# A four-layer graph network on one core: LSTM gates by tanh alone on rows of twice the size, norms of the last two groups on ScalarE, three planner times longer, last stores tile by tile

## The chip, the cores and the metric

The kernel runs on one core of a Trainium2 chip. The metric is the device time in microseconds (us) of one execution. A comparison can tell about 0.2% (5 us) from no change. A core has TensorE (PE: matmuls, with PEld for the loads of their weights), VectorE (DVE), ScalarE (ACT), GpSimd (POOL), and SyncE (SP), which here issues nearly all DMAs. Each engine works through its own instructions in order and waits at semaphores for the others.

## The reference

The input x is 128 batches of 64 nodes with 256 features, so 8192 rows; adj is one 64 x 64 matrix. Four layers follow, each of the form x = layernorm(x + layer(x)), all in float32. Layer 0 is three graph convolutions with weights adj * adj; layer 1 a spectral convolution with the eigenvectors of a normalized Laplacian of adj; layer 3 attention over neighbours. The change touches layer 2 above all: two graph convolutions with relu, and then LSTMs over windows of p = 1 to 4 nodes, one after the other on the same rows:

```python
def _lstm_last(Wih, Whh, bih, bhh, xs):          # xs [windows, p, H]
    def step(carry, x_t):
        h, c = carry
        g = x_t @ Wih.T + h @ Whh.T + bih + bhh
        i, f, gg, o = jnp.split(g, 4, axis=-1)
        c = jax.nn.sigmoid(f) * c + jax.nn.sigmoid(i) * jnp.tanh(gg)
        h = jax.nn.sigmoid(o) * jnp.tanh(c)
        return ((h, c), None)
...
for p in range(1, 5):
    nw = Tv // p
    wins = h[:, :nw * p, :].reshape(Bv * nw, p, Hd)
    last = _lstm_last(Wih[p - 1], Whh[p - 1], bih[p - 1], bhh[p - 1], wins)
    h = h.at[:, jnp.arange(nw) * p + (p - 1), :].set(last.reshape(Bv, nw, Hd))
```

## The kernel before

The 8192 rows are 64 tiles of 128 rows (two batches each), held in SBUF as X for the whole run. A group is four tiles; there are 16 groups. The first phase (to about 860 us) computes layer 0 for all groups while the eigenvectors are found on DVE in between. The second phase takes every group through layers 1, 2 and 3. The change lies in the second phase, apart from a scaling of the LSTM biases (cbi) at the seam.

In the second phase three groups are under way at any time (WAYS). Each is a generator: it issues some matmuls with what belongs to them on the other engines, and yields the time at which it may go on. This time is not measured; it is a statement: `now`, the planner's own count of TensorE time, plus a constant. The constants are at L920: MOVE for a copy out of PSUM, NORM for a norm, CELL for a step of the LSTM by its number of columns, SOFT for a softmax. The loop at the end of the kernel function (L1195) takes the first group whose time has come, and if none has, it moves `now` to the earliest one. TensorE's order is this order exactly. On the other engines a scheduler orders the instructions at build time, and the engine then keeps to that order.

The steps that the change touches:

- `lstm` (L989) computes gates transposed: 128 gate columns on the partitions, the windows of eight batches along the free dimension (256, 168 or 128 columns). Two halves h, and for each the gates i, f, g, o. Each gate is a few matmuls into PSUM and one ScalarE activation with the bias (L1027): sigmoid, or tanh for g. VectorE then forms the cell (L1031, L1032, L1034), ScalarE its tanh (L1035), VectorE the new hidden row (L1037, or L1046 back into hT at the last step).
- `layer2` (L1053) makes hT by a relu (L1073), runs the five LSTM calls, transposes back (L1089) and adds to X (L1090), two tiles at a time. A norm of the pair follows.
- `norm_parts` (L542) is the norm: statistics on VectorE (L551, L552), the inverse root as a power on GpSimd (L553, L554), and the application, on VectorE (L564). In the last two groups (ENDING, 14 and 15) every second tile is applied on ScalarE instead (L562), for which GpSimd forms a negated product (L557, L558).
- `layer3` (L1095) transposes X, copies it out of PSUM (L1114 or L1117, and L1118), multiplies by dw, transposes back, forms scores (L1140), softmax with an exp on ScalarE (L1153), attention times values, the sum into X (L1170), a norm, and the store by SyncE (L1174). In the last two groups layer 3 runs as two parts of two tiles.

ScalarE needs the table of a function loaded before it runs: an ACT_TABLE_LOAD in the trace. Nothing in the kernel asks for it; it is placed at build time.

Of the kernel before, what the change touches and what calls it, by code (L numbers as in the profile page):

```python
# [11 lines left out]
AF = mybir.ActivationFunctionType  # L12
ALU = mybir.AluOpType
# [525 lines left out]
LEAD = 10  # L539


def norm_parts(tc, pool, x, half, shared=False):  # L542


    nc = tc.nc
    n = x.shape[1]
    st = pool.tile([P, n, 6], F32, name="ln_st")
    mv = pool.tile([P, n, 2], F32, name="ln_mv")
    rs = pool.tile([P, n], F32, name="ln_rs")
    for t in range(n):  # L550
        nc.vector.bn_stats(st[:, t, :], x[:, t, :])  # L551
        nc.vector.bn_aggr(mv[:, t, :], st[:, t, :])  # L552
    nc.gpsimd.tensor_scalar(rs, mv[:, :, 1], EPS, None, op0=ALU.add)  # L553
    nc.gpsimd.tensor_tensor(rs, rs, half[:, :n], ALU.pow)  # L554
    if shared:
        nm = pool.tile([P, n], F32, name="ln_nm")
        nc.gpsimd.tensor_scalar(nm, mv[:, :, 0], -1.0, None, op0=ALU.mult)  # L557
        nc.gpsimd.tensor_tensor(nm, nm, rs, ALU.mult)  # L558
    yield
    for t in range(n):  # L560
        if shared and t % 2:
            nc.scalar.activation(x[:, t, :], x[:, t, :], AF.Identity, bias=nm[:, t:t + 1], scale=rs[:, t:t + 1])  # L562
            continue
        nc.vector.tensor_scalar(x[:, t, :], x[:, t, :], mv[:, t, 0:1], rs[:, t:t + 1],  # L564
                                op0=ALU.subtract, op1=ALU.mult)
# [22 lines left out]
            [lambda t=t: apply(t) for t in range(2)])  # L588


def rows_norm(tc, pool, x, half, shared=False):
    for _ in norm_parts(tc, pool, x, half, shared):
        pass


# [1 line left out]
def kernel(  # L597
# [296 lines left out]
    V.tensor_reduce(rs_col, adst, AX.X, ALU.add)  # L894
    V.tensor_scalar(wide["c_b0"], wide["c_b0"], rs_col, None, op0=ALU.mult)
    V.tensor_add(cbi, cbi, cbh)
    phase_a.close()
    us = keep.tile([P, 1], F32, name="us")
    ub2 = wide["b_b2"]
# [18 lines left out]

    now[0] = due[0] = 0.0
    MOVE, MIXED, LIN, CONV, NORM, SOFT = 1.2, 1.2, 1.5, 1.8, 5.2, 5.2  # L920
    CELL = {256: 3.3, 168: 2.2, 128: 1.9}

    def turn(out, in_):
        PE.transpose(out, in_, ident)  # L924
# [28 lines left out]
        yield now[0] + MIXED  # L953
        return dst

    def norm(xs, t, ready, more=0.0, shared=False):
        rows_norm(tc, small, xs[:, t:t + 2, :], half, shared)
        ready.append(now[0] + NORM + more)

    def layer1(xs, ready):  # L960
        a = yield from mixed(xs, u2, ready)
# [25 lines left out]
        return ready  # L987

    def lstm(hT, p, first, nw):  # L989


        n = 8 * nw
        wi, wh, bias = wih[p - 1], whh[p - 1], cbi[:, p - 1, :]
        c = hs = None
        for t in range(p):
            rows = slice(first + t, first + t + (nw - 1) * p + 1, p)
            xt = [hT[:, k, rows, :] for k in range(2)]
            last = t == p - 1
# [12 lines left out]
            if t:  # L1011
                yield ready
            if p > 1 and not t:
                c = tl(pg, [P, 512], "c")[:, :2 * n].rearrange("p (h n) -> p h n", h=2)
            new = None if last else tl(pg, [P, 512], "hs")[:, :2 * n].rearrange("p (h n) -> p h n", h=2)
            for h, q in units:
                j = 2 * "ifgo".index(q) + h
                m = slice(j * P, (j + 1) * P)
                pp = ahead.get((h, q))
                if pp is None:  # L1020
                    pp = ps4()[:, :n]
                    for k in range(2):
# [4 lines left out]
                S.activation(gate[q][:, h, :], pp, AF.Tanh if q == "g" else AF.Sigmoid, bias=bias[:, j:j + 1])  # L1027
                if q == "g":
                    to = gate["g"][:, h, :] if t or p == 1 else c[:, h, :]
                    if t:  # L1030
                        V.tensor_mul(c[:, h, :], c[:, h, :], gate["f"][:, h, :])  # L1031
                    V.tensor_mul(to, gate["i"][:, h, :], gate["g"][:, h, :])  # L1032
                    if t:
                        V.tensor_add(c[:, h, :], c[:, h, :], to)  # L1034
                    S.activation(gate["i"][:, h, :], c[:, h, :] if p > 1 else to, AF.Tanh)  # L1035
                if q == "o" and not last:
                    V.tensor_mul(new[:, h, :], gate["o"][:, h, :], gate["i"][:, h, :])  # L1037
                if q == "o":
                    if h == 0:
                        yield now[0]  # L1040
                elif h == 1 or len(units) == 8:
                    yield now[0]
            if last:

                for h in range(2):
                    V.tensor_mul(hT[:, h, slice(first + p - 1, first + nw * p, p), :],  # L1046
                                 gate["o"][:, h, :].rearrange("p (w b) -> p w b", b=8),
                                 gate["i"][:, h, :].rearrange("p (w b) -> p w b", b=8))
            ready = now[0] + CELL[n]
            hs = new  # L1050
        return ready

    def layer2(xs, g, ready):  # L1053
# [31 lines left out]
        for t in range(0, 4, 2):  # L1085
            p = ps4((P, 2, D))
            for j in range(2):
                for k in range(2):
                    turn(p[:, j, k * P:(k + 1) * P], hb[:, k, (t + j) * P:(t + j + 1) * P])  # L1089
            V.tensor_add(xs[:, t:t + 2, :], p, xs[:, t:t + 2, :])  # L1090
            norm(xs, t, ready, shared=g in ENDING)
            yield now[0]
        return ready

    def layer3(xs, g, ready, first, nt):  # L1095
# [20 lines left out]
            with tc.high_priority(offset=1500):  # L1116
                V.tensor_copy(xT[:, 0, :], ps[0][:, :nt * P])  # L1117
# [46 lines left out]
        for t in range(0, nt, 2):  # L1164
# [87 lines left out]
```

## Time and profile before

| | before |
|---|---|
| median of three runs | 2550.1 us (2548.05 to 2553.39) |
| the profiled execution | 2548.97 us, span 2547.2 us |
| granted TensorE clock | 0.996 |
| busy: PE, DVE, ACT, POOL | 98%, 56%, 44%, 5% |
| ACT_TABLE_LOAD | 31, 1.28 us each |
| output stores | 32 of 256 KB |

The span runs from the first to the last instruction. In the lines shown, a group or a timeline row gives the engine, the line of the kernel, the operation, the tile written and the tiles read; `[1.01 <-POOL ln_rs L554]` is idle time of the engine just before, and what ended it. A busy time of PE is the time in which some matmul is under way; records of matmuls overlap one another. In the list of waits the three numbers are the total in us, how often, and the longest.

### The profile page before, as it was taken

What the parts mean: (1) busy time and instruction counts of PE and PEld (TensorE: products, weight loads), DVE (VectorE), ACT (ScalarE), POOL (GpSimd) and SP (SyncE); (2) the same over time, 40 slices, a digit from 0 to 9 for tenths busy, and PEclk for the clock granted to TensorE, in tenths of its full rate; (3) what the DMA queues carried; (4) which work ended last, traced back from release to release, by engine and by line L of the source; (5) the groups of instructions that cost most, each with busy time, mean ns of one, the idle gap of its engine ahead of it and who ended that gap; (6) DMA issues with size and microseconds to landing.
All of it is one profiled execution on the core that took longest, in us unless ns stands there. A gap on an engine that the chain in (4) does not pass through costs nothing.

```text
span 2547.2 us, 38989 instructions
## 1 busy us (share of the span) xinstructions
PE 2495.1 (98%) x15020; PEld 2190.4 (86%) x15020; DVE 1414.6 (56%) x5002; ACT 1122.8 (44%) x2727; POOL 130.4 (5%) x316
## 2 busy tenths in 40 slices
PE   9999999999999999999999999999999999999996
PEld 7788887888878889988989889889898898988995
DVE  6888777778884433444453544534535445353335
ACT  2344333433333344545454454444444545445444
POOL 0000000000000100000000000000000000000001
PEclk9999999999999999999999999999999999999998
DMA  6000000000000300000000000000000000000000
GB/s 219 1 1 1 1 1 1 1 1 1 1 1 1 116 1 1 9 9 1 9 9 1 9 1 10 9 1 10 8 2 9 1 9 9 1 9 1 1 1 25
DMA packets 24570, 32.09 MB, mean 13 GB/s; under 512 B 2112, under 2 KB 21312, under 8 KB 24384
## 3 DMA queue, kind: packets, MB, share of 16 engines
q1 hardware_dynamic: 24032, 29.32, 3.4%
q8 instruction: 118, 1.93, 0.3%
q14 instruction: 68, 0.56, 0.1%
q10 hardware_dynamic: 352, 0.28, 0.0%
HBM read 21.20 MB, written 8.39 MB: 12 GB/s over the span
## 4 chain that ended last, share of the span: by engine, by line
PE 87%; DVE 6%; ACT 3%; POOL 2%; issue 1%; DMA 1%; SPq 0%; POOLq 0%; ACTq 0%; DVEq 0%
PE ps L716 84%; POOL ln_rs L554 1%; DVE X L564 1%; PE ps L924 1%; ACT gates L1027 1%; DVE D L51 1%; DVE ln_st L551 1%; PE ps L1140 1%; ACT L1027 1%; ACT L1153 1%; DVE X L1090 1%; PE pc L93 1%; DMA X<-in_x_dram 1%; ACT att L1153 0%; DVE gates L1032 0%
## 5 line engine op out<-in xcount | busy, mean ns | idle before, releaser
L716 PE MATMUL ps<-w,wih 128*128 128x128 f32 (+2 forms) x4992 | 894.1, 319 | 1.7 <-DVE w L1046 1.7
L716 PEld LDWEIGHTS ps<-w,wih 128*128 128x128 f32 x4992 | 763.8, 191 | 50.8 <-issue 8.4
L1027 ACT ACTIVATE gates<-ps,cbi 128x128 f32<-128x128 f32 (+2 forms) x1248 | 500.6, 408 | 581.1 <-PE ps L716 576.3
L716 PE MATMUL ps<-hs,whh 128*128 128x128 f32 (+2 forms) x3072 | 542.2, 303 | 4.4 <-DVE hs L1037 4.3
L716 PEld LDWEIGHTS ps<-hs,whh 128*128 128x128 f32 x3072 | 453.9, 191 | 33.7 <-issue 11.0
L1032 DVE TENSOR_TENSOR gates<-gates 128x128 f32<-128x128 f32 (+2 forms) x256 | 89.4, 349 | 253.9 <-ACT gates L1027 253.9
L716 PE MATMUL ps<-aw,h 128*128 128x256 f32 x1024 | 227.2, 380 | 0.0
L716 PEld LDWEIGHTS ps<-aw,h 128*128 128x128 f32 x1024 | 193.0, 190 | 25.8 <-ACT h L725 0.5
L725 ACT ACTIVATE h<-h 128x512 f32<-128x512 f32 x128 | 80.6, 629 | 169.4 <-DVE h L51 169.3
L1035 ACT ACTIVATE gates<-c 128x128 f32<-128x128 f32 (+2 forms) x288 | 98.1, 341 | 109.3 <-DVE c L1034 103.4
L1031 DVE TENSOR_TENSOR c<-c,gates 128x128 f32<-128x128 f32 (+2 forms) x192 | 62.4, 325 | 107.8 <-ACT gates L1027 105.5
L716 PE MATMUL ps<-ss,tw 128*128 128x256 f32 x512 | 117.9, 380 | 0.0
L716 PE MATMUL ps<-ss,aw 128*128 128x256 f32 x512 | 117.3, 379 | 0.0
L716 PE MATMUL ps<-m,aw 128*128 128x256 f32 x512 | 117.1, 380 | 0.0
L1046 DVE TENSOR_TENSOR w<-gates 128x256 f32<-128x256 f32 (+2 forms) x160 | 59.3, 377 | 101.8 <-PE ps L716 62.9
L716 PE MATMUL ps<-aw,m 128*128 128x512 f32 x256 | 114.5, 593 | 0.2 <-DMA aw<-in_a_w_dram 0.2
L1037 DVE TENSOR_TENSOR hs<-gates 128x128 f32<-128x128 f32 (+2 forms) x192 | 62.7, 327 | 92.0 <-ACT gates L1035 52.4
L564 DVE TENSOR_SCALAR X<-X,ln_mv,ln_rs 128x256 f32<-128x256 f32 x184 | 68.1, 410 | 81.6 <-POOL ln_rs L554 81.6
L716 PEld LDWEIGHTS ps<-ss,aw 128*128 128x128 f32 x512 | 96.6, 190 | 12.8
L716 PEld LDWEIGHTS ps<-ss,tw 128*128 128x128 f32 x512 | 96.4, 190 | 12.8 <-issue 0.2
L716 PEld LDWEIGHTS ps<-m,aw 128*128 128x128 f32 x512 | 95.7, 190 | 12.5 <-issue 0.5
L553 POOL TENSOR_SCALAR ln_rs<-ln_mv 128x2 f32<-128x2 f32 x96 | 22.8, 238 | 1569.4 <-DVE ln_mv L552 1567.6
(294 smaller groups left out, 3128.8 us busy)
## 6 DMA issues: line engine op xcount, KB each, us to landing
out_dram<-X SPq DMA_DIRECT2D x32, 256.0 KB, 2.1
X<-in_x_dram SPq DMA_DIRECT2D x30, 256.0 KB, 6.0
wih<-in_c_ih_dram SPq DMA_DIRECT2D x4, 1024.0 KB, 7.0
aw<-in_a_w_dram SPq DMA_DIRECT2D x3, 1024.0 KB, 10.8
whh<-in_c_hh_dram SPq DMA_DIRECT2D x3, 1024.0 KB, 9.1
aw<-in_a_w_dram SPq DMA_DIRECT2D x1, 512.0 KB, 6.3
cw<-in_c_w_dram SPq DMA_DIRECT2D x2, 256.0 KB, 5.1
X<-in_x_dram ACTq DMA_DIRECT2D x1, 256.0 KB, 3.6
```

The lines of the kernel that those rows point to most:

```text
L51: return getattr(self.engine, name)(out, *args, **kw)
L93: PE.matmul(out, lhsT, rhs, start=True, stop=True)
L551: nc.vector.bn_stats(st[:, t, :], x[:, t, :])
L564: nc.vector.tensor_scalar(x[:, t, :], x[:, t, :], mv[:, t, 0:1], rs[:, t:t + 1], op0=ALU.subtract, op1=ALU.mult)
L716: PE.matmul(out, lhsT, rhs, start=start, stop=stop)
L725: S.activation(dst, src, AF.Relu)
L1027: S.activation(gate[q][:, h, :], pp, AF.Tanh if q == "g" else AF.Sigmoid, bias=bias[:, j:j + 1])
L1031: V.tensor_mul(c[:, h, :], c[:, h, :], gate["f"][:, h, :])
L1032: V.tensor_mul(to, gate["i"][:, h, :], gate["g"][:, h, :])
L1035: S.activation(gate["i"][:, h, :], c[:, h, :] if p > 1 else to, AF.Tanh)
L1037: V.tensor_mul(new[:, h, :], gate["o"][:, h, :], gate["i"][:, h, :])
L1046: V.tensor_mul(hT[:, h, slice(first + p - 1, first + nw * p, p), :], gate["o"][:, h, :].rearrange("p (w b) -> p w b", b=8), gate["i"][:, h ...
```

## The change

Sigmoid is written as (1 + tanh(z/2))/2, so that all gates are tanh. To spare the extra operations, the rows in hT, the hidden rows and the cell are held at twice their value: the relu gets a scale of 2, the biases of i, f and o are halved once, the gates' scales are 0.25 (i, f, o) and 0.5 (g), the products on VectorE become one instruction of the form (a + 1) * b, and the last sum into X takes half. In the last two groups ScalarE applies every norm whose `scalar` is set (that of layer 2 and that of layer 3), both tiles of the pair; before, it took one of the two. Three stated times grow: CELL for 256 columns from 3.3 to 3.8, the second norm of a pair by 0.8 (and by another 1.8 in layer 2 of the last two groups), and the copy at the start of layer 3 by 0.6. The stores of the last two groups are one per tile.

```diff
@@ norm_parts
-    if shared:
+    if scalar:
         nm = pool.tile([P, n], F32, name="ln_nm")
...
-        if shared and t % 2:
+        if scalar:
             nc.scalar.activation(x[:, t, :], x[:, t, :], AF.Identity, bias=nm[:, t:t + 1], scale=rs[:, t:t + 1])
             continue
@@ seam
     V.tensor_add(cbi, cbi, cbh)
+    for q in (slice(0, 4), slice(6, 8)):
+        V.tensor_scalar(cbi[:, :, q], cbi[:, :, q], 0.5, None, op0=ALU.mult)
@@ stated times
-    CELL = {256: 3.3, 168: 2.2, 128: 1.9}
+    CELL = {256: 3.8, 168: 2.2, 128: 1.9}
...
-        ready.append(now[0] + NORM + more)
+        ready.append(now[0] + NORM + more + (0.8 if ready else 0.0))
@@ lstm
-                S.activation(gate[q][:, h, :], pp, AF.Tanh if q == "g" else AF.Sigmoid, bias=bias[:, j:j + 1])
+                S.activation(gate[q][:, h, :], pp, AF.Tanh, bias=bias[:, j:j + 1], scale=0.5 if q == "g" else 0.25)
...
-                        V.tensor_mul(c[:, h, :], c[:, h, :], gate["f"][:, h, :])
-                    V.tensor_mul(to, gate["i"][:, h, :], gate["g"][:, h, :])
+                        V.scalar_tensor_tensor(c[:, h, :], gate["f"][:, h, :], 1.0, c[:, h, :], op0=ALU.add,
+                                               op1=ALU.mult)
+                    V.scalar_tensor_tensor(to, gate["i"][:, h, :], 1.0, gate["g"][:, h, :], op0=ALU.add, op1=ALU.mult)
                     if t:
-                        V.tensor_add(c[:, h, :], c[:, h, :], to)
-                    S.activation(gate["i"][:, h, :], c[:, h, :] if p > 1 else to, AF.Tanh)
+                        V.scalar_tensor_tensor(c[:, h, :], c[:, h, :], 0.5, to, op0=ALU.mult, op1=ALU.add)
+                    S.activation(gate["i"][:, h, :], c[:, h, :] if p > 1 else to, AF.Tanh, scale=0.5)
                 if q == "o" and not last:
-                    V.tensor_mul(new[:, h, :], gate["o"][:, h, :], gate["i"][:, h, :])
+                    V.scalar_tensor_tensor(new[:, h, :], gate["o"][:, h, :], 1.0, gate["i"][:, h, :], op0=ALU.add,
+                                           op1=ALU.mult)
...
@@ layer2
-            relu(hT[:, c, :, :].rearrange("p n b -> p b n"), as3(h, 8))
+            S.activation(hT[:, c, :, :].rearrange("p n b -> p b n"), as3(h, 8), AF.Relu, scale=2.0)
...
-            V.tensor_add(xs[:, t:t + 2, :], p, xs[:, t:t + 2, :])
-            norm(xs, t, ready, shared=g in ENDING)
+            V.scalar_tensor_tensor(xs[:, t:t + 2, :], p, 0.5, xs[:, t:t + 2, :], op0=ALU.mult, op1=ALU.add)
+            norm(xs, t, ready, 1.8 if t and g in ENDING else 0.0, scalar=g in ENDING)
@@ layer3
-        yield now[0] + MOVE
+        yield now[0] + MOVE + 0.6
...
-            nc.sync.dma_start(out_t[:, at:at + 2, :], x2)
+            if ending:
+                for j in range(2):
+                    nc.sync.dma_start(out_t[:, at + j, :], x2[:, j, :])
+            else:
+                nc.sync.dma_start(out_t[:, at:at + 2, :], x2)
```

The last step's product into hT (L1046) changes in the same way as that of the hidden row.

More of the change, by code (lines that the diff above doesn't have):

```diff
@@ L539, with norm_parts @@
 LEAD = 10
-def norm_parts(tc, pool, x, half, shared=False):
+def norm_parts(tc, pool, x, half, scalar=False):
     nc = tc.nc
@@ L588, in scalar_norm, with rows_norm @@
             [lambda t=t: apply(t) for t in range(2)])
-def rows_norm(tc, pool, x, half, shared=False):
-    for _ in norm_parts(tc, pool, x, half, shared):
+def rows_norm(tc, pool, x, half, scalar=False):
+    for _ in norm_parts(tc, pool, x, half, scalar):
         pass
@@ L954, in mixed, with norm @@
         return dst
-    def norm(xs, t, ready, more=0.0, shared=False):
-        rows_norm(tc, small, xs[:, t:t + 2, :], half, shared)
-        ready.append(now[0] + NORM + more)
+    def norm(xs, t, ready, more=0.0, scalar=False):
+        rows_norm(tc, small, xs[:, t:t + 2, :], half, scalar)
+        ready.append(now[0] + NORM + more + (0.8 if ready else 0.0))
     def layer1(xs, ready):
@@ L1045, in lstm @@
                 for h in range(2):
-                    V.tensor_mul(hT[:, h, slice(first + p - 1, first + nw * p, p), :],
-                                 gate["o"][:, h, :].rearrange("p (w b) -> p w b", b=8),
-                                 gate["i"][:, h, :].rearrange("p (w b) -> p w b", b=8))
+                    V.scalar_tensor_tensor(hT[:, h, slice(first + p - 1, first + nw * p, p), :],
+                                           gate["o"][:, h, :].rearrange("p (w b) -> p w b", b=8), 1.0,
+                                           gate["i"][:, h, :].rearrange("p (w b) -> p w b", b=8), op0=ALU.add,
+                                           op1=ALU.mult)
             ready = now[0] + CELL[n]
```

## The prediction

> **What bounds the kernel now.** I read the busy table and the slices of the page first, then the table by stretches, then who TensorE waited for, then the timeline around those waits.
>
> ```profile
> PE 2495.1 (98%) x15020; PEld 2190.4 (86%) x15020; DVE 1414.6 (56%) x5002; ACT 1122.8 (44%) x2727; POOL 130.4 (5%) x316
> ...
> 1400.00:1600.00 200.00, 197.70 (x1336) 179.52 (x1335) 90.98 (x255) 94.66 (x230) 10.43 (x22) 1.00 0.02 6
> 2500.00:2547.00 47.00, 25.58 (x163) 19.62 (x161) 24.65 (x88) 15.32 (x36) 8.88 (x26) 0.79 0.10 34
> ```
>
> TensorE is the bound from end to end; DVE and ACT have half their time free in the middle. Only what makes TensorE wait counts, and the end, where it is idle nearly half of the time. The columns of the stretches are PE, PEld, DVE, ACT, POOL, granted clock, DMA share, GB/s.
>
> ```profile
> PE ps L924 <- DVE X L564: 11.2, 11, 5.3
> PE ps L924 <- ACT att L1153: 4.8, 4, 2.4
> PE ps L716 <- DVE hs L1037: 4.3, 11, 1.5
> PE ps L716 <- DVE w L1117: 3.9, 9, 0.4
> ```
>
> [...] A matmul's record overlaps the wait, so I took the price of a wait from the starts of the matmuls in the trace: the distance to the next start, less the median distance of that width (0.112 us for 128 columns, 0.216 for 256, 0.429 for 512). So counted, TensorE loses 58.9 us: 15 before 900 us (the change hardly touches that), 21.9 from 900 to 2400, and 22.3 after 2400. Another 10.6 us lie between the last matmul group (2536.6) and the end of the span. From 1300 to 2230 us the loss repeats every 103.3 us (one group of four tiles): 0.66 on X by L564 (layer 3 transposes its second pair of tiles), 0.60 on w by L1117 (the copy after them), 0.38 on hs by L1037 (recurrent matmuls of 256 columns). Nine of each: 5.9 + 5.4 + 3.4 = 14.7 us.
>
> **Part 1, one table for all (the gates).** At 1116 to 1121 us the timeline has:
>
> ```profile
> 1117.81 0.84 ACT L1153 ACTIVATE att<-v 64x256 f32<-64x256 f32 x2
> 1118.67 0.42 ACT L1035 ACTIVATE gates<-c 128x256 f32<-128x256 f32 x1
> ...
> 1119.11 1.28 ACT L1027 ACT_TABLE_LOAD   x1
> ...
> 1120.40 0.47 ACT L1027 ACTIVATE gates<-ps,cbi 128x256 f32<-128x256 f32 x1
> 1120.91 0.42 DVE L1046 TENSOR_TENSOR w<-gates 128x256 f32<-128x256 f32 x1 [1.33 <-ACT gates L1027]
> ...
> 1121.39 0.84 PE L716 MATMUL ps<-w,wih 128*128 128x168 f32 x4 [1.68 <-DVE w L1046]
> ```
>
> The tanh of L1035 runs straight after the exp of L1153, with no load; the load comes with the next sigmoid of L1027. So tanh and exp live in one table, and without sigmoid the 15 loads at L1027 and 15 at L1153 fall to one: 29 x 1.283 = 37.2 us of ACT. Of this only what TensorE waited for is worth time. Here the load sits on the path: TensorE lost 1.84 us. The same chain stands behind 0.95 us at 1029.4 (load at 1026.12, then a gate, a relu and the eT copy of L1160) and behind each repeating 0.38 (load at 1417.86, gate at 1419.15, hs at 1419.66, TensorE at 1420.14). All are smaller than 1.28 except the first: 1.3 + 0.95 + 3.4 = 5.6, taken as 5.5.
> The Trainium skill (ScalarE: Activation LUTs, What ACT_TABLE_LOAD costs) puts a switch at about 2.66 us, the load and a drain of 1.38. The trace differs: at 2484.27 a gate ends, the load runs from 2484.28 to 2485.56, the exp starts at 2485.58. So 1.3 a switch. By the page the loads hold ACT for 77 us and not 37, which would explain stalls twice as long as those seen; I keep the trace.
> Per element a tanh costs what a sigmoid does as far as the rows show: L1027 is one row of both, 470 ns at 256 columns. The scales are immediates of instructions that exist already. On DVE about 1,120 TENSOR_TENSOR (the lines L1031 to L1046 and L1090) become SCALAR_TENSOR_TENSOR with an immediate. Bounds: nothing (the 64x64 rows have 211 ns against 214), or +55 ns as with a per-partition scalar (L1071 746 against L1061 691), 61 us of DVE that is 45% busy there. The nearer row is the one with an immediate, so 0; the other end puts 0.2 us on a step of the recurrence, inside its allowance. The two scalings of cbi are under 0.3 us each, at the seam near 860 us, long before a gate reads them: 0.
>
> **Part 2, three stated times.** They move nothing in the hardware; they change which group's matmuls TensorE takes next. +0.8 for the second norm of a pair answers the 0.66, MOVE + 0.6 answers the 0.60, CELL 3.8 for 3.3 answers the 0.38. While the planner holds a group back, two others fill TensorE, so a longer time costs nothing where another is able. But every later choice moves too: the order of the evacuations on DVE and ACT, and the psum and work buffers they free. Of 5.9 + 5.4 I take 70%, 8 us: bounds 11.3 and, with new waits of the same size, 0 or below.
>
> **Part 3, the end.** Columns of the timeline: start, length, instruction, in brackets the idle time before it.
>
> ```profile
> 2540.06 0.41 DVE L564 TENSOR_SCALAR X<-X,ln_mv,ln_rs 128x256 f32<-128x256 f32 x1 [1.01 <-POOL ln_rs L554]
> 2540.11 0.19 POOL L558 TENSOR_TENSOR ln_nm<-ln_nm,ln_rs 128x2 f32<-128x2 f32 x1
> 2540.34 0.60 ACT L562 ACTIVATE X<-X,ln_nm,ln_rs 128x256 f32<-128x256 f32 x1 [5.08 <-POOL ln_nm L558]
> 2540.39 0.74 DVE L551 BATCH_NORM_STATS2 ln_st<-X 128x6 f32<-128x256 f32 x2
> ```
>
> DVE's apply waits 1.01 us for POOL at the head of DVE's queue, and the next pair's statistics, whose data were there at 2539.05, start behind it. Now 8 applies (4 norms of layer 2, 4 of layer 3) leave DVE for ACT. POOL already issues its four instructions for these norms: +0. Cost: ACT's second apply comes some 0.5 us after the first (0.60 less overlap), and it needs nm, 0.24 us later than rs. Queued behind it on ACT are the gates of the other group and the next copies; ACT waits there for nm already, for the odd tile, so only the 0.5 is new.
> A rule speaks against it: ScalarE: Activation LUTs, Rules for kernel authors, wants multiplies and adds on VectorE. The rows agree on the price of one, 600 against 410 ns: by the rule 8 x 0.19 = 1.5 us are lost. But what ends the wait is the queue, not the duration:
> Last norm: statistics 1.34 earlier, then POOL bounds (first pair's nm ends at 2540.30, 1.46 for the next: 2541.8 against 2543.26), 1.4 earlier; +0.5 for the second apply; the last store moves half the bytes (256 KB went from 2544.8 to 2545.7: -0.45). SP gets 4 more DMA issues of 0.37, beside the second apply, and about 0.1 more closing waits. Net -1.2.
> Second pair of group 15 before layer 3: TensorE lost 5.48 at 2522.9. Its statistics (2519.78) stood behind two such applies (2516.25, 2519.45). Without them POOL bounds: three norms from 2515.03 at 1.46 end at 2519.4, the applies at 2520.0 and 2520.5 against 2522.8 and 2523.25: 2.8 earlier. And the planner, told +0.8 +1.8, now lets the first pair's dw matmuls (8 of 16, which took 5.1 us behind the transposes) go into the wait: another 1.2. Together -4.
> Loads in the tail: 2508.15 (TensorE lost 2.56) and 2484.28 with 2486.77 (lost 1.29): of these -2. Tail: 1.2 + 4 + 2 = 7.2.
>
> **Sum.** 5.5 + 8 + 7.2 = 20.7 us. The profiled execution took 2548.97 (span 2547.2, 1.8 around it): 2528.3. It stood 1.1 under the median of the three runs, so 2529.
>
> **Rivals.**
> A, the new order gives back what it takes: the 8 us are 0, other waits appear. For it: the waits at 1131.2 (1.67, hs behind L564 on DVE) and 2259.4 (2.48, w by L951 behind L564) show that DVE's queue is not in the planner's times. 2529 + 8 = 2537.
> B, the tail keeps its length: TensorE's order makes the second pair's chain start later, or ACT, with applies at the head of its queue, delays gates and exps: only 1 of 7.2 is left: 2535. For it: ACT waited 20.8 us in all for nm there, 8 times. Against: it had 5 us idle before the last ones.
> C, slower: the longer times lock the three groups into a repeating order in which two of the six norms of a group meet DVE's queue badly, as at 1131.2. Price 2 x 1.67 a group, ten groups: 33 us; less the 20.7: 2529 + 33 = 2562. It decides from 2.1 us of new wait a group. Against: the old order had only one repeating wait on L564, of 0.66.
> D, the loads stay, because the table of the first tanh lacks exp: the trace excludes it but for the choice made for the first one. Then 2529 + 7 = 2536.
>
> **Numbers.** Main case 0.56, A 0.2, B 0.12, D 0.02, C 0.06, and 0.04 for a mixture that ends at no change. [...] Faster 0.90, same 0.04, slower 0.06. Low end: all of the middle's 21.9 and half of the tail's 22.3 gone, 33: 2517. High end 2545: A and B together (2543) and the upper DVE price.
>
> **What would show it.** One or two ACT_TABLE_LOAD after the root's, and ACT some 37 us less busy. Waits of TensorE on w by L1117 and on hs by L1037 gone, those on X by L564 small in the middle; the windows of 200 us at 199 or more. L562 with 16 instead of 8 applies, L564 with 176; in the tail no DVE wait in front of statistics. PE's and POOL's busy time unchanged. Wrong: a repeating wait per group above 2 us, or a last stretch from 2400 us on as long as now.

## The result, and the profile after

| | before | after |
|---|---|---|
| median of four runs each | 2549.26 us (2548.05 to 2553.39) | 2540.14 us (2536.74 to 2541.67) |
| ratio | | 0.996 [0.9942, 0.9977] |
| profiled execution, span | 2548.97, 2547.2 | 2536.74, 2534.9 |

The change makes the kernel 9.1 us faster, where 21 was forecast. The profiled execution is the fastest of the four. It falls 12.3 us short of the span before; the sum had wanted 20.7.

The busy table and two stretches of the kernel after (columns of the stretches as before: PE, PEld, DVE, ACT, POOL, granted clock, DMA share, GB/s):

```profile
PE 2491.7 (98%) x15020; PEld 2188.7 (86%) x15020; DVE 1411.0 (56%) x4996; ACT 1094.8 (43%) x2706; POOL 133.1 (5%) x316
...
1400.00:1600.00 200.00, 197.28 (x1330) 179.37 (x1331) 91.13 (x257) 89.78 (x226) 10.85 (x23) 1.00 0.02 6
2500.00:2534.00 34.00, 19.61 (x138) 15.02 (x136) 18.61 (x66) 14.68 (x35) 7.97 (x24) 0.79 0.10 32
```

ACT was busy 28 us less: the 29 loads of 1.283 that went are 37.2, but the applications are busy 3.9 longer (8.7 for 4.8) and the gates 1.1; some 4 us are left without an explanation. The end is shorter: from 2500 us on 34.9 us are left where there were 47.2. But the stretch in the middle is no better: PE 197.28 of 200, where it was 197.70.

Groups of the kernel after, with the tables and the applications on ScalarE:

```profile
L562 ACT ACTIVATE X<-X,ln_nm,ln_rs 128x256 f32<-128x256 f32 x16 | 8.7, 592 | 9.5 <-POOL ln_nm L558 7.2 <-DVE ln_st L551 2.3
L674 ACT ACT_TABLE_LOAD x1 | 1.3, 1283 | 2.2 <-issue 2.2
L1030 ACT ACT_TABLE_LOAD x1 | 1.3, 1283 | 0.0
L1036 DVE SCALAR_TENSOR_TENSOR gates<-gates 128x256 f32<-128x256 f32 (+2 forms) x256 | 89.6, 350 | 294.6 <-ACT gates L1030 294.6
```

Two loads are left in the whole run: the root's and one for the gates. The product of the gates costs 350 ns with its immediate, 349 before.

What TensorE waited for in the kernel after, from 850 us on (total, times, longest). Lines have moved: L926 is the transpose that was L924, L1159 the exp (L1153), L1041 the hidden row (L1037), L1123 the copy in layer 3 (L1117), L953 the copy that was L951.

```profile
PE ps L926 <- DVE X L564: 17.2, 22, 1.1
PE ps L716 <- ACT v L1166: 3.3, 3, 2.0
PE ps L926 <- ACT att L1159: 3.2, 2, 1.8
...
PE ps L716 <- DVE hs L1041: 0.8, 1, 0.8
```

The repeating waits on w by the copy and on hs are gone, as forecast. Those on X by L564 were to get small; they doubled in number, from 11 to 22, and hold 17.2 us.

From here on TensorE's loss is counted by stages that are bounded by the same work in every kernel: the middle from about 919 to 2300 us, the tail from 2450 us to the last matmul group, and the piece behind that. The count is that of the prediction, from start to start. It is a net one (starts that come sooner than the median are set against the waits), so the single waits of a kernel can add up to more than its middle.

| us lost | middle | tail | behind the last matmuls |
|---|---|---|---|
| before | 22.1 | 22.5 | 9.6 |
| after | 20.4 | 14.6 | 7.9 |

So 9.6 of the 12.3 us came from the end and 1.7 from the middle; the remaining 1.0 lies ahead of the middle.

### The profile page after: what moved, and what is told of

Its sections match the earlier page's. It is cut to its first block, busy times and chain, and to the rows that moved or that the text cites. A ratio compares the mean times of both kernels' runs of the same rounds, so it can differ in the third digit from the quotient of the medians.

```text
span 2534.9 us, 38990 instructions
## 1 busy us (share of the span) xinstructions
PE 2491.7 (98%) x15020; PEld 2188.7 (86%) x15020; DVE 1411.0 (56%) x4996; ACT 1094.8 (43%) x2706; POOL 133.1 (5%) x316
## 4 chain that ended last, share of the span: by engine, by line
PE 93%; DVE 5%; POOL 1%; issue 1%; ACT 0%; DMA 0%; SPq 0%; ACTq 0%; POOLq 0%; DVEq 0%
PE ps L716 90%; PE ps L926 2%; POOL ln_rs L554 1%; DVE D L51 1%; DVE X L564 1%; DVE X L1096 1%; PE ps L1146 1%; PE pc L93 1%; DVE ln_st L551 1%; DVE tw L51 0%; POOL ln_rs L553 0%; DVE ln_mv L552 0%; DVE h L51 0%; DVE u L51 0%; DMA X<-in_x_dram 0%
## 5 line engine op out<-in xcount | busy, mean ns | idle before, releaser
L716 PE MATMUL ps<-w,wih 128*128 128x256 f32 (+2 forms) x4992 | 895.3, 319 | 0.0
L716 PEld LDWEIGHTS ps<-hs,whh 128*128 128x128 f32 x3072 | 453.0, 191 | 17.2 <-issue 1.7
L1036 DVE SCALAR_TENSOR_TENSOR gates<-gates 128x256 f32<-128x256 f32 (+2 forms) x256 | 89.6, 350 | 294.6 <-ACT gates L1030 294.6
L1034 DVE SCALAR_TENSOR_TENSOR c<-gates,c 128x128 f32<-128x128 f32 (+2 forms) x192 | 62.6, 326 | 117.7 <-ACT gates L1030 117.4
L1041 DVE SCALAR_TENSOR_TENSOR hs<-gates 128x128 f32<-128x128 f32 (+2 forms) x192 | 62.8, 327 | 89.1 <-ACT gates L1039 51.5
L564 DVE TENSOR_SCALAR X<-X,ln_mv,ln_rs 128x256 f32<-128x256 f32 x176 | 64.8, 410 | 81.0 <-POOL ln_rs L554 81.0
L1051 DVE SCALAR_TENSOR_TENSOR w<-gates 128x256 f32<-128x256 f32 (+2 forms) x160 | 59.5, 378 | 90.1 <-PE ps L716 61.0
```

What stands on the lines that cost most here:

```text
L716: PE.matmul(out, lhsT, rhs, start=start, stop=stop)
L1034: V.scalar_tensor_tensor(c[:, h, :], gate["f"][:, h, :], 1.0, c[:, h, :], op0=ALU.add, op1=ALU.mult)
L1036: V.scalar_tensor_tensor(to, gate["i"][:, h, :], 1.0, gate["g"][:, h, :], op0=ALU.add, op1=ALU.mult)
L1041: V.scalar_tensor_tensor(new[:, h, :], gate["o"][:, h, :], 1.0, gate["i"][:, h, :], op0=ALU.add, op1=ALU.mult)
L1051: V.scalar_tensor_tensor(hT[:, h, slice(first + p - 1, first + nw * p, p), :], gate["o"][:, h, :].rearrange("p (w b) -> p w b", b=8), 1.0, ...
```

## The experiments

Every kernel was timed beside the kernel before, in 5 to 20 executions; the median of before was 2552.1 to 2553.1 us. A gain in us is the distance of the ratio from 1, times that median.

| kernel | ratio to before | median | middle, as traced | drops of the clock in it | middle without them | tail | behind |
|---|---|---|---|---|---|---|---|
| e1_gates | 0.9955 [0.9942, 0.9967] | 2540.76 | 16.1 | 1 | 14.4 | 19.3 | 9.7 |
| e2_times | 0.9976 [0.9966, 0.9985] | 2545.13 | 20.2 | 0 | 20.2 | 20.6 | 9.7 |
| e3_tail | 0.998 [0.9973, 0.9987] | 2547.58 | 25.5 | 2 | 22.1 | 19.5 | 8.1 |
| e4_no_times | 0.9935 [0.9922, 0.9947] | 2535.07 | 16.0 | 1 | 14.3 | 16.0 | 8.0 |
| after_again | 0.9956 [0.9943, 0.9968] | 2540.35 | 20.4 | 0 | 20.4 | 16.4 | 8.2 |
| a1_old_cell | 0.9933 [0.9921, 0.9946] | 2536.22 | 16.2 | 0 | 16.2 | 14.0 | 8.0 |
| e5_tail_times | 0.993 [0.9918, 0.9943] | 2534.89 | 16.0 | 1 | 14.3 | 15.6 | 8.2 |
| b1_moved | 0.9936 [0.9922, 0.995] | 2534.21 | 18.3 | 1 | 16.6 | 13.8 | 8.0 |
| e6_loads | 1.002 [1.0012, 1.0029] | 2556.93 | 20.2 | 0 | 20.2 | 31.0 | 9.7 |
| e7_no_scalar | 0.9952 [0.9939, 0.9964] | 2540.19 | 16.1 | 1 | 14.4 | 19.8 | 8.9 |
| b2_split | 0.9936 [0.9922, 0.9949] | 2535.92 | 15.4 | 1 | 13.7 | 16.9 | 8.0 |
| b3_spaced | 0.9921 [0.9907, 0.9934] | 2531.27 | 7.6 | 0 | 7.6 | 19.6 | 8.2 |

The drops belong to single executions and not to a kernel; they are told of at the end, and each costs 1.7 us. The profiled execution of before had none in its middle.

### The parts, each alone

e1_gates is the kernel before with the gates by tanh and nothing else.

```diff
-  S.activation(gate[q][:, h, :], pp, AF.Tanh if q == "g" else AF.Sigmoid, bias=...)
+  S.activation(gate[q][:, h, :], pp, AF.Tanh, bias=..., scale=0.5 if q == "g" else 0.25)
...
```

> The kernel before with the gates by tanh alone (rows twice as large, all scales), nothing else of the change. TensorE's order is that of before. Theory T (the loads on TensorE's path are worth their waits, the stated times are worth nothing in the middle): the waits of 1.84 at 1121, 0.95 at 1029 and the repeating 0.38 on hs go, the repeating 0.66 and 0.60 stay, and about 2 us go in the tail: 7 us less, ratio 0.997. Rival R (the loads are hidden behind other groups, and the change's gain comes from the times and the tail): under 2 us, ratio 1.000.

Measured: 11.5 us faster (0.9955), more than the 7 expected; 14.4 in the middle instead of 22.1. The repeating wait on hs and the lone ones at 1029 and 1121 are gone. What TensorE waited for from 900 to 2450 us:

```profile
PE ps L926 <- DVE X L564: 4.6, 9, 0.5
PE ps L716 <- DVE w L1123: 3.9, 9, 0.4
PE ps L716 <- DVE w L953: 2.4, 1, 2.4
PE ps L716 <- DVE hs L1041: 1.5, 1, 1.5
```

By the spans of the profiled executions the gain is 8.2. The rest comes from the execution of before that was profiled: at 2548.97 us it lies 3.4 under the median of before.

e2_times is before with the three stated times.

```diff
-    CELL = {256: 3.3, 168: 2.2, 128: 1.9}
+    CELL = {256: 3.8, 168: 2.2, 128: 1.9}
-        ready.append(now[0] + NORM + more)
+        ready.append(now[0] + NORM + more + (0.8 if ready else 0.0))
-            norm(xs, t, ready, shared=g in ENDING)
+            norm(xs, t, ready, 1.8 if t and g in ENDING else 0.0, shared=g in ENDING)
-        yield now[0] + MOVE
+        yield now[0] + MOVE + 0.6
```

> The kernel before with the three stated times alone (CELL 3.8, second norm +0.8 and +1.8, MOVE + 0.6). The prediction's step: 8 us less, the repeating waits on X and w gone. Theory T (with the longer times all three groups are held back at once, TensorE has nothing to take): X waits of 1.25 and 0.64 in every group as in the kernel after, so nothing gained in the middle (0 to 3 us more, hs waits by table loads included), and 2 to 3 us gained in the tail by the other order: within 3 us of before, ratio 0.999 to 1.001.

Measured: 6.1 us faster (0.9976), so the expected "within 3 us of before" was missed, and the 8 of the prediction too. In the profile the gain is 1.9 in the middle and 1.9 in the tail, and the expected waits on X are there, 22 of them, 17.2 us in all, as in the kernel after. The timed gain is larger mainly because of the executions that were profiled: that of before lies 3.4 us under its median, at a mean clock of 0.996 where the executions at 0.994 took 2552.8 us and more, and that of e2_times lies 1.0 above its own.

e3_tail is before with the applications of the last two groups on ScalarE and the stores tile by tile.

```diff
-        if shared and t % 2:
+        if shared:
-            nc.sync.dma_start(out_t[:, at:at + 2, :], x2)
+            if ending:
+                for j in range(2):
+                    nc.sync.dma_start(out_t[:, at + j, :], x2[:, j, :])
+            else:
+                nc.sync.dma_start(out_t[:, at:at + 2, :], x2)
```

> The kernel before with ScalarE applying both tiles in the norms of the last two groups and the last stores tile by tile; times and gates as before. The prediction's step: last norm -1.2, second pair of group 15 -2.8, so 4 us less, ratio 0.9984; the wait of 5.5 us before layer 3's last transposes falls to under 3. Rival: ACT's queue delays gates and exps of the other group by as much; no change (1.000).

Measured: 5.1 us faster (0.998): 3.0 in the tail and 1.5 behind the last matmuls. The longest wait ahead of layer 3's last transposes is 2.4, as expected.

e4_no_times is after with the three old times, so e1 and e3 together.

```diff
-    CELL = {256: 3.8, 168: 2.2, 128: 1.9}
+    CELL = {256: 3.3, 168: 2.2, 128: 1.9}
-        ready.append(now[0] + NORM + more + (0.8 if ready else 0.0))
+        ready.append(now[0] + NORM + more)
-            norm(xs, t, ready, 1.8 if t and g in ENDING else 0.0, scalar=g in ENDING)
+            norm(xs, t, ready, scalar=g in ENDING)
-        yield now[0] + MOVE + 0.6
+        yield now[0] + MOVE
```

> The kernel after with the three stated times put back to those of before (gates, ScalarE norms and stores stay). Theory T: the middle has the old repeating waits of 0.66 and 0.60 (1.26 a group) in place of 1.25 and 0.64 (1.89), so 6 us less in the middle than the kernel after, and 2 to 3 us lost in the tail by the old order: 2536 to 2539, ratio to before 0.9955. Rival R (the times carry the gain): within 3 us of before, ratio 0.999.

Measured: 2535.07 us, 0.9935: 16.6 faster than before, which is 11.5 and 5.1. Gates and tail add up. The kernel without the longer times beats the one with them.

### The change again, and one time less

after_again is the changed kernel, unaltered.

> The kernel after, unchanged, beside the others of this call on one chip: ratio 0.996 as before. Theory T reads it against e4_no_times: the two orders differ by 0.0025, and this run should stand above the three others of this call.

Measured: 0.9956 against the 0.9935 of e4: the three times cost 5.4 us once the gates are tanh. In the profiles the middle has 20.4 against 14.3. With the old gates it was 20.2 (e2_times) against 22.1: with the longer times the middle loses the same, whichever the gates.

a1_old_cell takes only CELL back.

```diff
-    CELL = {256: 3.8, 168: 2.2, 128: 1.9}
+    CELL = {256: 3.3, 168: 2.2, 128: 1.9}
```

> The kernel after with CELL for 256 columns put back from 3.8 to 3.3; the second norm's +0.8 and +1.8 and MOVE + 0.6 stay. Theory C (CELL alone aligns the three groups so that all are held back at once: the planner's own count then finds nothing able for 1.50, 0.64 and 0.32 in each group; with 3.3 it finds nothing able for one stretch of 0.90): one repeating wait of about 0.9 in place of 1.25 + 0.64, some 9 us less than after, ratio 0.9925. Rival N (the longer norm times themselves make the X waits): they stay at 1.9 a group, ratio 0.996.

Measured: 0.9933, a little short of the 0.9925 expected. Nearly all of the loss was CELL's: the middle falls from 20.4 to 16.2; the other two times keep some 2 us by the profile, too little for the timing to show. Which of those two holds them was not tried. A single wait a group is left, as expected, but on w and not on X, and 1.76 by the starts in place of 0.9. What TensorE waits for in a1_old_cell from 850 to 2450 us, and its timeline at one group:

```profile
PE ps L716 <- DVE w L1123: 14.4, 9, 1.6
...
1499.41 1.03 PE L716 MATMUL ps<-w,wih 128*128 128x256 f32 x4
1500.28 0.60 PE L926 MATMUL ps<-ident,X 128*128 128x128 f32 x4
...
1503.37 3.67 PE L716 MATMUL ps<-w,dw 128*128 128x512 f32 x8 [1.59 <-DVE w L1123]
```

The waits on X are gone in this kernel: its transposes start without one. Directly behind them, in the same group, TensorE waits 1.59 us for the copy of the very tile it has just transposed. A wait that is taken away here comes back one step later, because there is still nothing else to run. The kernel after shows the first half of the same, at 1292 us, beside the same place of the kernel before, at 1394:

```profile
1292.33 1.04 PE L926 MATMUL ps<-ident,w 128*128 128x128 f32 x8
1293.20 1.89 PE L716 MATMUL ps<-w,wih 128*128 128x256 f32 x8
...
1294.93 1.05 PE L716 MATMUL ps<-ut,v 128*128 128x128 f32 x8
...
1297.07 0.67 PE L926 MATMUL ps<-ident,X 128*128 128x128 f32 x4 [1.08 <-DVE X L564]
...
1299.08 0.76 PE L926 MATMUL ps<-ident,X 128*128 128x128 f32 x4 [0.47 <-DVE X L564]
```

```profile
1394.43 1.04 PE L924 MATMUL ps<-ident,w 128*128 128x128 f32 x8
1395.31 5.35 PE L716 MATMUL ps<-w,wih 128*128 128x256 f32 x24
1400.49 0.60 PE L924 MATMUL ps<-ident,X 128*128 128x128 f32 x4
...
1401.59 0.77 PE L924 MATMUL ps<-ident,X 128*128 128x128 f32 x4 [0.50 <-DVE X L564]
```

Between layer 2's last transposes back and layer 3's first, the norms of that group have to pass. Before, 24 gate matmuls of another group lay there, 5.2 us. After, 8 gate matmuls and 8 of layer 1 are all that is able, 2.6 us; then the planner has all three groups held. So TensorE takes the transposes and waits for them.

This can be followed in the planner's own sums, worked through with its stated times (a count of statements, not of time). In the repeating part they have all three groups held at once, in every group, for 0.11 us with the times of before, for 1.50, 0.64, 0.12 and 0.32 with those of after, for 0.90 and 0.11 with CELL back at 3.3, and for 0.11, no more than before, with the times of b1_moved below. The trace of after shows two waits a group, 1.25 and 0.64 us, in 11 groups: 20.8 us, or nearly all that was lost in its middle.

### Where longer times are harmless

e5_tail_times keeps the longer times for the last two groups alone.

```diff
-            norm(xs, t, ready, 1.8 if t and g in ENDING else 0.0, scalar=g in ENDING)
+            norm(xs, t, ready, 2.6 if t and g in ENDING else 0.0, scalar=g in ENDING)
-        yield now[0] + MOVE + 0.6
+        yield now[0] + MOVE + (0.6 if ending else 0.0)
```

The other two times are the old ones.

> The kernel after with the longer times in the last two groups alone (second norm of layer 2 there +2.6, layer 3's copy there +0.6); CELL, the other norms and copies as before. Theory T: the middle as in e4_no_times (waits of 0.66 and 0.60), the tail as in after, where TensorE and the stretch behind it lost 22.5 us against 24.0: 1 to 2 us less than e4_no_times, ratio 0.993. Rival: the middle and the tail can't be had apart, the tail's order depends on how the groups stand when the last one starts: within 1 us of e4_no_times or above.

Measured: 0.993, the same as e4_no_times within its interval; of the 1 to 2 us expected from the tail the profile shows 0.4 (15.6 for 16.0). The middle is e4_no_times's to the tenth. Two waits remain a group, as in the kernel before: X by L564, 0.66 by the starts, and w by L1123, 0.60.

b1_moved adds small times that, by the planner's sums, hold all three groups at once no longer than the times of before do: CELL 3.5, MOVE + 0.6, and no longer second norms but in the last two groups.

```diff
-    CELL = {256: 3.8, 168: 2.2, 128: 1.9}
+    CELL = {256: 3.5, 168: 2.2, 128: 1.9}
-        ready.append(now[0] + NORM + more + (0.8 if ready else 0.0))
+        ready.append(now[0] + NORM + more)
-            norm(xs, t, ready, 1.8 if t and g in ENDING else 0.0, scalar=g in ENDING)
+            norm(xs, t, ready, 2.6 if t and g in ENDING else 0.0, scalar=g in ENDING)
```

> The kernel after with other stated times: CELL 3.5, MOVE + 0.6 kept, no +0.8 for the second norms but in layer 2 of the last two groups (+2.6). By the planner's own count nothing is held back in the middle (0.99 us in all against 27 in after). Theory C: the waits on w by L1123 go, those on X by L564 stay at 0.66 a group, about 6 us less than e4_no_times, ratio 0.991. Rival (every order has its own waits of about 1.3 a group, whatever the planner counts): as e4_no_times, 0.9935.

Measured: 0.9936. The main expectation missed, the rival held. The two repeating waits are those of e5_tail_times, in the waits from 850 to 2450 us of b1_moved and then of e5_tail_times:

```profile
PE ps L926 <- DVE X L564: 5.7, 11, 0.6
PE ps L716 <- DVE w L1123: 4.4, 10, 0.4
```

```profile
PE ps L926 <- DVE X L564: 4.5, 9, 0.5
PE ps L716 <- DVE w L1123: 3.9, 9, 0.4
```

With MOVE + 0.6 the order of the matmuls at that place was the same as without. In these kernels an addition to a stated time does nothing until it is long enough to let another group in, and then it moves whole runs of matmuls. A small count in the planner's sums does not promise that the waits go, either: 0.11 us a group stands against 1.26 of waits. At these two waits TensorE had taken the step because its stated time was up, and the data came later.

b2_split goes at the wait itself: in layer 2 the statistics of both pairs are queued ahead of the first application on DVE (the times are those of e5_tail_times).

```diff
+        parts = []
...
-            norm(xs, t, ready, ...)
+            parts.append(norm_parts(tc, small, xs[:, t:t + 2, :], half, g in ENDING))
+            with tc.high_priority(offset=1500):
+                next(parts[-1])
+            if t:
+                for part in parts:
+                    next(part, None)
+            ready.append(now[0] + NORM + ((2.6 if g in ENDING else 0.0) if t else 0.0))
```

> e5_tail_times with layer 2's norm in two parts: the statistics of both pairs of tiles first (at high priority), then the applications, so that no application waiting for GpSimd stands in front of the second pair's statistics on VectorE. TensorE's order and all stated times are those of e5_tail_times. Theory H: X of the second pair comes about 1 us earlier, the repeating wait of 0.66 on it goes, in ten groups 6 us: ratio 0.9905. Rival F (what TensorE lacks there is other work, so a wait removed comes back at the next step of the same group): the wait on w by L1123 grows from 0.60 by as much, ratio 0.993.

Measured: 0.9936, no gain. By the starts of the matmuls the wait on X fell from 0.66 to 0.27 and that on w rose from 0.60 to 0.94: 1.26 became 1.21. It is a1_old_cell over again.

### What fills TensorE

b3_spaced changes not a single time of the kernel after, only which of several able groups is taken while groups are still to come: not always the oldest, but the one with the fewest steps, 20 steps being allowed for each place in the order of the groups.

```diff
-                pick = able[0] if todo else min(able, key=lambda x: x[1] + LEAD * x[3])
+                pick = min(able, key=lambda x: x[1] + (20 if todo else LEAD) * x[3])
```

> The kernel after, all of its stated times kept, with one line of the planner changed: while groups are still to come it no longer takes the first in its list that is able, but the one with the smallest count of steps done plus 20 times its number. So the three groups stay some 20 steps apart and do not come to their norms, copies and softmaxes together. Theory F (TensorE waits where all three groups stand at once; the stated times are about right, and what lacks is other work at those points): by the planner's own count the middle has no stretch left in which nothing is able (27 us in after), so most of the 20.4 us lost up to 2300 us go: 12 to 18 us less than after, 2523 to 2530, ratio 0.988 to 0.992. Rival (every order ends with 16 to 20 us of waits in the middle, since the engines behind TensorE set them): ratio 0.993 to 0.996.

Measured: 0.9921, 2531.27 us (2529.56 to 2531.73), the fastest of all and 9.1 us under after_again, short of the 12 to 18 expected. The middle loses 7.6 instead of 20.4 with the very times of after, and the planner's sums with this rule never have three groups held at once in it. The same rule with the old times was not run, so what the times alone do under it is not shown; nor does the run part the distance between the groups from whatever else the new order changed. Waits of b3_spaced from 900 us on, and its stretch from 1400 to 1600 us:

```profile
PE ps L716 <- DVE w L953: 7.0, 12, 0.6
PE ps L926 <- ACT X L562: 3.5, 1, 3.5
PE ps L716 <- DVE hs L1041: 3.2, 2, 2.7
...
1400.00:1600.00 200.00, 198.84 (x1324) 181.52 (x1321) 91.73 (x263) 94.13 (x231) 11.05 (x24) 1.00 0.02 6
```

The waits on X by L564 and on w by L1123 are gone together, and none took their place there. A smaller one has come elsewhere, once a group, on the copy L953 (0.74 by the starts). DVE's queue is behind it, at 1457 us of the same kernel:

```profile
1457.61 0.74 DVE L564 TENSOR_SCALAR X<-X,ln_mv,ln_rs 128x256 f32<-128x256 f32 x2 [1.13 <-POOL ln_rs L554]
1458.26 0.68 DVE L953 COPY w<-ps 128x512 f32<-128x512 f32 x1
...
1459.00 1.55 PE L716 MATMUL ps<-w,cw 128*128 128x512 f32 x3 [0.58 <-DVE w L953]
```

The copy that TensorE waits for stands behind an application that waited 1.13 us for POOL. The tail of this kernel, 19.6, is worse than after's; a rule for the last groups to go with it was not tried.

### The loads and the applications, each put back

e6_loads is e1_gates with one sigmoid of a single column behind each exp, which brings the loads back.

```diff
+        S.activation(small.tile([P, 1], F32, name="idle"), e[:, 0, 0:1], AF.Sigmoid)
```

> e1_gates (gates by tanh, order of before) with one activation more in each layer 3, a sigmoid of one column behind the exps, into a tile that nothing reads. It brings the table loads back, two in each of the 18 passes of layer 3, and changes nothing else: all gates are still tanh. Theory T (the loads are the cause of what e1_gates gained, 0.9955): the waits on hs of 0.38 and the lone ones near 1029 and 1121 come back, and the time with them: 0.999 to 1.000. Rival (the gain is in the instructions: the form of the gates and of the products on VectorE): it stays at 0.9955 to 0.997.

Measured: 1.002, 16.2 us slower than e1_gates and slower than expected. Groups, then waits from 900 us on:

```profile
L1160 ACT ACT_TABLE_LOAD x18 | 23.1, 1283 | 0.3
L1159 ACT ACT_TABLE_LOAD x17 | 21.8, 1283 | 0.3
...
PE ps L926 <- ACT att L1159: 10.5, 5, 3.0
PE ps L716 <- DVE hs L1041: 4.0, 11, 1.5
```

The repeating wait on hs is back (4.0, 11 times; it was 4.3, 11 times), and the middle went from 14.4 to 20.2, by 5.8 us. The lone wait near 1121 is back as well, the one near 1029 is not. Nothing but the loads and the tiny sigmoids was added. The tail went from 19.3 to 31.0, more than the old loads had cost it: each load here follows the exp at once, so the next part's exp finds the wrong table every time.

e7_no_scalar is e4_no_times with VectorE applying one tile of each pair again; the stores stay.

```diff
-        if scalar:
+        if scalar and t % 2:
```

> e4_no_times (old times, new gates) with the norms of the last two groups shared as before, every second tile on VectorE; stores tile by tile stay. Theory H (VectorE's apply stood at the head of its queue waiting for GpSimd, and the next statistics behind it): the wait before layer 3's last transposes is 5.5 again in place of 2.4 and 2.6, and the last norm ends about 1 us later: 4 us more than e4_no_times, ratio 0.995. Rival (the stores gave the end its gain): within 1 us of e4_no_times.

Measured: 0.9952 against 0.9935, 4.3 us. Its timeline at the second pair of group 15:

```profile
2511.39 0.41 DVE L564 TENSOR_SCALAR X<-X,ln_mv,ln_rs 128x256 f32<-128x256 f32 x1 [1.02 <-POOL ln_rs L554]
2511.72 0.74 DVE L551 BATCH_NORM_STATS2 ln_st<-X 128x6 f32<-128x256 f32 x2
...
2514.87 1.08 PE L926 MATMUL ps<-ident,X 128*128 128x128 f32 x4 [5.08 <-DVE X L564]
```

The wait of 5.08 us is back, and ahead of it the statistics behind an application that waited for POOL. In e4_no_times the two transposes of that kind wait 2.19 and 2.39 us. The stores alone, which e7_no_scalar has and e1_gates has not, shorten the piece behind the last matmuls from 9.7 to 8.9; the applications take it to 8.0.

## Why the prediction was right in sign and too large in size, by its own steps

**Part 2 failed.** Its term was 8 us gained, from "While the planner holds a group back, two others fill TensorE, so a longer time costs nothing where another is able". The condition at the end of that sentence does not hold: with CELL at 3.8 all three groups are held together once and again in every group. The middle with the new gates alone is 14.4, with the times on top 20.4: 6.0 lost where 8 was to be gained. Of the three waits aimed at, those on w and on hs went; that on the second pair of X stayed at 0.64 for 0.66, and one of 1.25 on the first pair came to it. Where the waits on X do shrink, in a1_old_cell and b2_split, the wait comes back at the next step of the same group; only b3_spaced, whose order gives TensorE something to run, makes the sum much smaller. The bound "0 or below" in the text was where it lay. On the old gates alone (e2_times) the same times gained 6.1 timed and 1.9 in the middle: there the wait on hs existed, which a longer CELL answers. With the loads gone that wait is gone already (e1_gates), and CELL answers nothing.

**Part 1 was right in mechanism, and larger.** Said: 5.5 in the middle and 2 in the tail. Measured: 7.7 in the middle of e1_gates (22.1 to 14.4), 3.2 in the tail, 11.5 timed. The lone wait at 1121 went whole, 1.84, where only 1.3 was counted; the waits named in the prediction make 6.2 of the 7.7, and the rest was not followed up. The load takes 1.28 us, as kept from the trace. DVE's new instruction costs 350 ns for 349: the lower bound was the right one.

**Part 3 was right in the main.** Said for the last norm: 1.2. The piece behind the last matmuls fell by 1.5 in e3_tail and 1.7 in after. The end of after shows why:

```profile
2528.26 0.74 DVE L551 BATCH_NORM_STATS2 ln_st<-X 128x6 f32<-128x256 f32 x2
...
2529.62 1.09 ACT L562 ACTIVATE X<-X,ln_nm,ln_rs 128x256 f32<-128x256 f32 x2 [3.45 <-POOL ln_nm L558]
2529.77 0.22 POOL L553 TENSOR_SCALAR ln_rs<-ln_mv 128x2 f32<-128x2 f32 x1 [0.18 <-issue]
...
2531.27 1.09 ACT L562 ACTIVATE X<-X,ln_nm,ln_rs 128x256 f32<-128x256 f32 x2 [0.55 <-POOL ln_nm L558]
```

The second pair's statistics run before the first pair is applied, and POOL goes on to it 0.18 us after the first. Two applications end 1.09 us after the first starts, so the second adds 0.5, as said. The second pair of group 15 was to give 4; e7_no_scalar puts the applications as a whole at 4.3. Of that 4, the 1.2 that the longer times were to add is not shown: the tail is 14.6 and 16.4 in two executions with them and 16.0 without. The rule that wants multiplies on VectorE would have had 1.5 us lost.

**The sum.** Middle 13.5 said, 1.7 found; tail and end 7.2 said, 9.6 found in the profile of after, and 7.5 in that of after_again. The two executions of one program differ by 1.8 in the tail, and this is the clock. Just ahead of the last eight matmuls they are in step to 0.1 us, apart from a drop of the clock in after_again near 890 us; these eight ran at a granted clock of 0.50 in after_again and of 1.00 in after. The last four of each, after_again first:

```profile
2528.99 2.08 PE L716 MATMUL ps<-w,v 128*128 128x256 f32 x4 [0.52 <-ACT v L1166]
```

```profile
2526.23 1.13 PE L716 MATMUL ps<-w,v 128*128 128x256 f32 x4 [0.52 <-ACT v L1166]
```

The four before them took 2.07 and 1.13. So 1.9 of the 9.6 was the luck of that execution.

**The rivals.** A, the new order gives back what it takes, happened and went further, and for a reason that the prediction did not name: it looked for DVE's queue. Its 2537 lies 3 us under the median, since the times took 6 more. B is refuted by the tail. C had the form right, an order that repeats with two waits by L564 in every group, at 1.89 a group instead of 3.3, but not the reason: at 1293 us of after the norms run through and no other group has matmuls to take. Against the 1.89 stood the 1.64 that went. Its point of decision, 2.1 us of new wait a group, was missed by a little. D is refuted: two loads.

**Signs.** Right: the loads, hs and w by the copy gone, 16 applications on L562, no wait of DVE in front of statistics at the end. Wrong: X by L564 small, the stretches of 200 us at 199, and ACT 37 us less busy: it was 28, and the eight applications (3.9) that the change itself puts on ACT had been left out of that figure.

## What to carry to other kernels

A stated latency in a hand-planned interleave is worth something only if another stream has work at that moment. Before making one longer, count through the order how often all streams are held at once; if they are, the wait moves to the next step, and the remedy that helped here is the distance between the streams, not the latency. A count near nothing is no proof that TensorE will not wait. Try such settings again after every change that shortens a chain: times tuned on the old gates gained 6 us there and cost 5 on the new ones. At an end with little left to run, take the instruction that waits at the head of a queue off that queue, even to an engine that is slower at it.

## What the runs showed of the hardware

The granted clock drops to half for 3.4 us behind some lone waits and not behind others of the same length. The same place in before and e3_tail, stretches of 3 us, the first line from before:

```profile
1123.00:1126.00 3.00, 3.00 (x19) 2.79 (x18) 2.54 (x9) 1.05 (x4) 0.00 (x0) 1.00 0.00 0
```

```profile
1123.00:1126.00 3.00, 3.00 (x12) 2.81 (x11) 0.33 (x1) 1.43 (x4) 0.00 (x0) 0.50 0.00 0
```

Both had just waited 1.68 us for the same w (until 1121.4 and 1122.5); e3_tail then runs 12 matmuls where before runs 19. Another lone wait, on the copy L951 (L953), in before and in e4_no_times:

```profile
2259.40 3.72 PE L716 MATMUL ps<-cw,w 128*128 128x256 f32 x16 [2.32 <-DVE w L951]
```

```profile
2251.91 5.41 PE L716 MATMUL ps<-cw,w 128*128 128x256 f32 x16 [2.42 <-DVE w L953]
```

The same 16 matmuls take 1.69 us longer. So a lone wait can cost 1.7 us more than its length, and PE stays "busy" meanwhile.

What decides is where the wait falls. In each of the 14 traces the granted clock changes only at points that lie whole multiples of 3.413 us apart, up to the end of the run (the drops of e3_tail at 1122.8 and 2262.9 are 334 of them apart). Here is the stretch of e3_tail between two such points that holds the wait, and then the two of before:

```profile
1119.42:1122.83 3.41, 1.54 (x11) 1.12 (x10) 1.29 (x3) 3.36 (x6) 0.00 (x0) 1.00 0.00 0
```

```profile
1117.53:1120.94 3.41, 1.99 (x15) 1.55 (x13) 1.04 (x4) 3.33 (x7) 0.00 (x0) 1.00 0.00 0
1120.94:1124.36 3.42, 2.97 (x17) 2.82 (x18) 1.31 (x4) 2.33 (x6) 0.00 (x0) 1.00 0.00 0
```

In e3_tail the whole wait lies in one stretch; in before a point cuts it in two. By the starts of the matmuls (gaps of more than 0.2 us over the median) TensorE was idle for 2.20 us in that stretch of e3_tail, and for 1.75 in the first of before. Counted so from 400 us to the last matmuls of all traces, every one of the 40 stretches at full clock with 2.18 us or more of idle TensorE is followed by one at 0.50. Of ten with 1.88 to 1.99 five are, and of some 8,600 with less none. The two waits of after add up to 1.89 a group, spread over some 3 us, and its middle has no drop.

e3_tail has two such drops in its middle, and without them exactly the 22.1 of before, as it should, since its edit lies at the end. a1_old_cell's five runs fall in two clusters by this: spans of 2529.7 and 2530.3 at a mean clock of 0.998, and 2534.4 to 2535.0 at 0.995 or 0.996. The Trainium skill (TensorE: Matmul & The Clock Gate, What's actually happening) has the gate judge free-running windows of about 3.4 us; the points 3.413 us apart agree with that. Its limit for gaps, about 3 us (Why this matters for your kernels), does not hold in these runs: 2.2 us of idle time within one window were enough.
